# An AdaLN block with sorted experts: grouping of the last batches, v projection layout, transfers per step, and order of the maximum's scores

## The chip, the cores and the metric

The kernel runs on one core of a Trainium2 chip. The metric is the device time of one execution in microseconds (us). The kernel before has a median of 872.28 us over 9 runs (868.27 to 878.45).

## The reference

For 16 batches of 512 tokens with 128 features, in float32, the block computes an adaptive layer norm, windowed attention, a second adaptive layer norm and a mixture of experts:

```python
h = layernorm(x) * (1 + ca) + sa            # ca, sa, ga, cb, sb, gb: per batch, from silu(c) @ wmod
x = x + ga * attention(h)                   # 16 heads of 8, keys within +-32 of the query, softmax
h = layernorm(x) * (1 + cb) + sb
scores = softmax(h @ gate_w.T)              # 8 experts, the best 2 of each token
routed = sum over the 2 of w2[e]( silu((s*h) @ w1[e]) * ((s*h) @ w3[e]) )
shared = ( silu(h @ w1s) * (h @ w3s) ) @ w2s
x = x + gb * (shared + routed)
```

## The kernel before

One instruction stream per engine is written out by hand, in the order in which the Python code emits it (a manual schedule). The main loop has 64 steps, four per batch; step (b, u) handles 128 queries.

**A step** does this. `weights` makes the transposed scores t (key by query) of this step in two PSUM tiles, and ScalarE (ACT) takes their exponential. `average` multiplies the weights of the step before with the values (`v_own`) into the unused columns of a score tile. `transposed(n + 1)` turns the next step's shifts (`neg`). `look_ahead(n + 3)` calls `row_max`: it computes the query-by-key scores s for the step three ahead, VectorE (DVE) takes their maximum (L402), and GpSimd (POOL) cuts it into three bf16 pieces (L410, L412). `divided` turns the average (`raw`, L471) and divides it. Between these calls, `between(b, u, 0..3)` puts in everything else by a table `places`: the projections of batch b+2 (`project`), the values of batch b+1 (`project_v`), the output projection, second norm, logits and shared expert of the batches before (`finish`, seven stages), and the three beats of the expert stream.

**PSUM.** t, s and the experts' `uv` tiles rotate through one pool of three tiles (`ps_s`); a new tile takes the one that came free first.

**Sorted experts.** The batches of a group (`GROUPS`, three at a time) are routed together (`route`): each token's two choices get positions in a table in HBM that is sorted by expert, in tiles of 128 rows. `scatter` writes the scaled rows there with indirect transfers issued by POOL, 8 per batch. The table is then worked off in quads of four tiles (`quads_of`: 8 quads for three batches, 6 for two, 4 for one). A quad has five parts: SyncE (SP) fetches its rows (`xg`, 256 KB) and four times one expert's matrices (`wg`, 4 x 192 KB); `beat_a` turns the rows (xT); `beat_b` multiplies them with w1 and w3 (`uv`) and gates; `beat_c` multiplies with w2 (`ye`) and stores the result from ACT's queue. Two quads are fetched ahead; `wg` and `xg` have three buffers each, so that a fetch waits for the `ye` or the xT of the quad three before. When a group's last quad is done, `combine` gathers the results, 8 indirect transfers per batch (`yg`, four buffers), adds them to what `finish` has stored, and stores the sum (L824).

**Budget of indirect transfers.** `window` lets POOL issue two pairs of transfers per step, scatters first. The first transfer of a window waits until ACT has copied `raw` of this step, so that the transfers of a step follow each other in one run.

**Unsorted batches.** Batches 14 and 15 are in no group: `scores_of` spreads their scores, and each of their units is one expert over all 512 tokens (`scaled`, `gated`, `added`): 9 units per batch, the shared expert among them.

**The tail.** After the last step a loop works in rounds: one quad and one unit per round, two calls of `tick` (finishing, routing, four indirect transfers, one call of `combining`). A round's order on TensorE (PE) is xT of the next quad, the unit's broadcast of scores (b), uv of this quad, uv of the unit (`uv_all`), ye of the quad before, `sums` of the unit before.

**Values.** `project_v` makes, for each of eight blocks of 64 queries, the values of 128 keys that begin 64 after each other: eight matmuls of 128 rows per batch, each row of keys computed twice. Two ACT copies per batch (L369) spread them into `v_own`.

Of the kernel before, what the change touches and what calls it, by code (L numbers as in the profile page):

```python
# [10 lines left out]
F32 = mybir.dt.float32  # L11
# [21 lines left out]
EPS = 1e-5  # L33
SCALE = DH ** -0.5
NEG = -1e30
GROUPS = (3, 3, 3, 3, 2)
SORTED = sum(GROUPS)
MAX_T = 4 * max(GROUPS)
QUAD = 4
# [11 lines left out]
def adaln_block(ctx: ExitStack, tc: tile.TileContext, x, wq, bq, wk, bk, wv, bv, wo, bo,  # L51
# [92 lines left out]
    pieces_of = [const.tile([P, 4, G, 32], BF16, name=f"pieces{n}") for n in range(NPC)]  # L144


    NVO = 3
    v_own_of = [const.tile([P, 2, 4 * 8 * 32 + 16], F32, name=f"v_own{n}") for n in range(NVO)]
    smallT = const.tile([P, 27], F32, name="smallT")
    modT = const.tile([P, 6, B], F32, name="modT")  # L150
    wT = [const.tile([P, D], F32, name=f"wT{n}") for n in range(4)]
# [23 lines left out]
    with ExitStack() as c1:  # L175
# [5 lines left out]
        def misc(name):  # L181
            return ps_m.tile([P, 512], F32, tag="m", name=name)
# [65 lines left out]
        def zero_but_ones(t):  # L248
            nc.gpsimd.memset(t, 0.0)
            nc.gpsimd.memset(  # L250
                t[:, :, 0 : 4 * 8 * 32].rearrange("p s (m c) -> p s m c", c=32)[:, :, :, DH : DH + 1], 1.0
            )

        def operands():
# [5 lines left out]
        def more_operands():  # L260
            for t in pieces_of[2:]:
                nc.gpsimd.tensor_copy(t.rearrange("p i g r -> p (i g r)"), pieces_0)
            zero_but_ones(v_own_of[2])
            nc.gpsimd.memset(zero, 0.0)

        def gate(t, shape, name):
# [90 lines left out]

        def project_v(b):

            m = made[b]  # L360
            hT = m.hT
            m.v_own = []
            for half in range(2):
                ps = misc(f"v_{b}_{half}")
                for n in range(4):
                    i = half * 4 + n
                    mm(ps[:, n * D : (n + 1) * D], hT[:, i * QB : i * QB + P], wvT)
                t = v_own_of[(2 * b + half) % NVO]
                nc.scalar.copy(  # L369
                    t[:, :, 0 : 4 * 8 * 32].rearrange("p s (m c) -> p m s c", c=32)[:, :, :, 0:DH],  # L370
                    ps.rearrange("p (m s c) -> p m s c", s=2, c=DH),
                )
                m.v_own += [(t.rearrange("p s c -> p (s c)"), 8 * n) for n in range(4)]
                yield

        def edge(u):
# [72 lines left out]
        def average(b, u, w, v_own):  # L449

            t = spare.pop() if spare else ps_s.tile([P, 2, 512], F32, tag="s", name=f"o_{b}_{u}")
            spare.clear()
            w = w.rearrange("p g (a h j q) -> p g a h j q", a=2, h=2, j=J)
            for a in range(2):
                c = slice(4 * KM + a * QB, 4 * KM + (a + 1) * QB)
                v, m0 = v_own[2 * u + a]
                for s in range(2):
                    for n in range(2):
                        for g in range(G):
                            k0 = s * 4 * 8 * 32 + (m0 + 2 * g + n) * 32  # L460
                            mm(t[32 * g : 32 * g + 32, n, c], v[:, k0 : k0 + 32], w[:, g, a, :, 2 * n + s, :],
                               start=s == 0, stop=s == 1)
            raw = wk_p.tile([P, 2, U], F32, tag="raw", name=f"raw_{b}_{u}", bufs=2)
            nc.scalar.copy(raw, t[:, :, 4 * KM : 4 * KM + U])
            return raw
# [233 lines left out]
        def scatter(g):  # L699


            r = sorts[g]
            r.stored = []

            def scaled_rows(b, k):

                rows = wk_p.tile([P, NT, D], F32, tag="rows", name=f"rows_{b}_{k}", bufs=2)
                n0 = (b - first_of[g]) * NT
                nc.vector.tensor_tensor(
                    rows, h2_of[b], r.top[:, k, n0 : n0 + NT].unsqueeze(2).to_broadcast([P, NT, D]), ALU.mult  # L710
                )
                return rows

            todo = [(b, k) for b in range(first_of[g], first_of[g] + GROUPS[g]) for k in range(2)]
            ahead = scaled_rows(*todo[0])
            yield
            for i, (b, k) in enumerate(todo):
                rows, n0 = ahead, (b - first_of[g]) * NT
                for t in range(NT):
                    while t % 2 == 0 and not two_free():  # L720
                        yield

                    nc.gpsimd.memset(apart, 0.0)
                    stored = nc.gpsimd.indirect_dma_start(  # L724
                        out=table[g % 2][:, :],
                        out_offset=bass.IndirectOffsetOnAxis(ap=r.pos[:, k, n0 + t : n0 + t + 1], axis=0),
                        in_=rows[:, t, :], in_offset=None,
                    ).ins
# [7 lines left out]
        sorts, scatters = {}, []  # L736
        n_places, window = [0], []

        def two_free():

            if not window:
                return False
            raw = window.pop()
            if raw is not None:
                nc.gpsimd.tensor_copy(apart, raw[0:1, 0, 0:1])
            return True
# [47 lines left out]
        def combined(g, b):  # L794

            r = sorts[g]
            ys = []
            for k in range(2):
                y = None
                for t in range(NT):  # L800
                    while t % 2 == 0 and not two_free():
                        yield
                    if y is None:
                        y = wk_p.tile([P, NT, D], F32, tag="yg", name=f"yg_{b}_{k}", bufs=4)
                    s = (b - first_of[g]) * NT + t
                    nc.gpsimd.indirect_dma_start(  # L806
                        out=y[:, t, :], out_offset=None, in_=result[g][:, :],
                        in_offset=bass.IndirectOffsetOnAxis(ap=r.pos[:, k, s : s + 1], axis=0),
                    )
# [12 lines left out]
            yield  # L822
            yield
            nc.sync.dma_start(out=x_dram, in_=xb)  # L824

        def combine(g):

            active, todo, n = [], list(range(first_of[g], first_of[g] + GROUPS[g])), 0
            while active or todo:
                if todo and n % 4 == 0:  # L830
                    active.append(combined(g, todo.pop(0)))
                n += 1
                active = [a for a in active if next(a, 0) is None]
                yield
# [34 lines left out]
            nc.vector.tensor_tensor(flat, ps, flat, ALU.add)  # L869
            nc.sync.dma_start(out=out[b].rearrange("(t p) d -> p t d", p=P), in_=xs[b])  # L870

        every, sums = [], []

        FETCH = 2
        stream = [(g, q) for g, nb in enumerate(GROUPS) for q in range(quads_of(nb))]
# [100 lines left out]
        def between(b, u, n):  # L976
            for f in places.get((u, n), []):
                f(b)
            if n < 3 or b == B - 1:
                routing()  # L980
            if n == 0 and raw_of:
                window[:] = [None, raw_of[-1]]
                scattering()
                combining()
                window.clear()
            n_places[0] += 1
            fetch_some()
# [16 lines left out]
        with tc.manual_schedule():  # L1004
# [21 lines left out]
            for n, (b, u) in enumerate(steps):  # L1026
# [7 lines left out]
                transposed(n + 1)  # L1034
                other_half()
                between(b, u, 0)
                if pending is not None:
                    divided(pending, raw)
                if n == 0:
                    projecting(1)  # L1040
                between(b, u, 1)
                if n == 0:
                    projecting(1)
                look_ahead(n + AHEAD)
                between(b, u, 2)
                if n < 3:
                    next(once, None)
# [11 lines left out]
            sums += [t[:, n, :] for n in range(2)]  # L1059
            x_next = h_last = None  # L1060
            stores = []

            def tick():
                for b in range(B - 3, B):
                    finishing(b)
                routing()
                window[:] = [None, None]
                scattering()
                combining()
                window.clear()  # L1070
                n_places[0] += 2
                fetch_some()
# [102 lines left out]
```

## Time and profile before

| | |
|---|---|
| median of 9 runs | 872.28 us |
| the profiled execution: its own time, its span | 875.78 us, 873.7 us |
| PE, DVE, ACT, POOL busy | 699.8, 442.7, 423.3, 426.1 us |
| mean granted TensorE clock | 0.909 |
| last step's t scores on PE | from 689.9 us |
| matmuls of the last quad's `ye` | at 832.3 us |
| last indirect transfer, last store | at 865.5 us, 870.3 us |

Times in the views are microseconds from the start of the span; a line like L402 is a line of the kernel's file. L62 is the helper through which all matmuls go, so its groups are told apart by their tiles. An arrow `a <- b` in a tile name reads "a is written from b"; `[3.6 <-X]` behind an instruction is the idle time of its engine before it and what ended it. "Another core or an unknown queue" and "remote" stand where the profile sees no releaser.

### The profile page before, as it was taken

The numbers are of one execution on the slowest core, as the hardware profiler recorded it, in microseconds if no ns is written. First come the engines' busy times: TensorE is split into PE (matmuls) and PEld (weight loads), VectorE is DVE, ScalarE is ACT, GpSimd is POOL, SyncE is SP. The second block draws the span as 40 slices with busy tenths as digits, with TensorE's granted clock in tenths as the row PEclk, the third lists the DMA queues.
The fourth block names the chain that finished last, engine by engine and source line by source line (L and its number), as shares of the span: only waits on it lengthen the run. The fifth ranks groups of instructions, "written<-read, shape, count | busy, mean of one in ns | idle before, by whom it ended". The sixth has DMA issues, their size and how long they took to land.

```text
span 873.7 us, 26167 instructions
## 1 busy us (share of the span) xinstructions
PE 699.8 (80%) x10792; PEld 524.2 (60%) x10792; DVE 442.7 (51%) x1058; ACT 423.3 (48%) x733; POOL 426.1 (49%) x934
## 2 busy tenths in 40 slices
PE   5889999877898888988988897788977655786980
PEld 3567676655676666766766776576765543554630
DVE  3444656744558253447635254653536452754482
ACT  3667777554675454745554555444542412332310
POOL 3533334486533555446556564454464647333355
PEclk9899999999999898998899899887997778898896
DMA  5080310112423524360553345345414344666634
GB/s 166 2 228 26 89 31 14 47 32 66 127 73 87 145 82 133 89 174 25 148 151 107 109 126 149 95 109 149 119 54 133 111 154 123 183 198 192 199 108 110
DMA packets 119509, 97.49 MB, mean 112 GB/s; under 512 B 9124, under 2 KB 113486, under 8 KB 119390
## 3 DMA queue, kind: packets, MB, share of 16 engines
q1 hardware_dynamic: 91834, 70.70, 29.1%
q0 software_dynamic: 7168, 14.69, 5.8%
q10 hardware_dynamic: 20388, 10.43, 4.1%
q8 instruction: 84, 1.38, 0.6%
q14 instruction: 35, 0.29, 0.1%
HBM read 66.39 MB, written 30.97 MB: 111 GB/s over the span
## 4 chain that ended last, share of the span: by engine, by line
PE 47%; DVE 14%; issue 14%; ACT 10%; another core or an unknown queue 6%; POOL 4%; DMA 2%; SPq 1%; DVEq 0%; ACTq 0%; POOLq 0%
PE s L62 12%; PE t L62 10%; PE uv L62 5%; DVE neg L402 3%; ACT w L444 2%; PE q L62 2%; POOL yg L806 2%; PE uv_sh L62 2%; PE ye L62 2%; PE lg L62 2%; PE v L62 2%; PE raw L471 2%; PE ys L62 2%; PE xT L211 2%
## 5 line engine op out<-in xcount | busy, mean ns | idle before, releaser
L444 ACT ACTIVATE w<-t 128x1024 f32<-128x1024 f32 x128 | 131.6, 1028 | 77.0 <-PE t L62 74.4
L806 POOL DMA_INDIRECT yg<-result,r_posi x112 | 110.6, 987 | 92.1 <-DVE yg L819 45.5
L402 DVE TENSOR_REDUCE neg<-s 128x8 f32<-128x768 f32 x128 | 116.7, 952 | 56.5 <-remote 22.0
L410 POOL CAST pieces<-neg 128x16 bf16<-128x16 f32 x192 | 56.1, 292 | 161.8 <-DVE neg L402 151.6
L724 POOL DMA_INDIRECT table<-rows,r_posi x112 | 112.3, 1002 | 26.3 <-issue 25.5
L62 PEld LDWEIGHTS s<-w,v_own 128*32 128x32 f32 x3904 | 67.2, 119 | 44.4 <-issue 31.3
L62 PE MATMUL s<-w,v_own 128*32 128x64 f32 x3904 | 81.1, 234 | 9.9 <-issue 9.6
L62 PE MATMUL t<-q_own,kT 32*128 32x256 f32 x1024 | 84.0, 437 | 0.0
L62 PEld LDWEIGHTS <-packed 32*128 32x128 bf16 (+2 forms) x1101 | 33.0, 97 | 82.8 <-issue 67.0
L62 PE MATMUL uv<-xT,wg 128*128 128x128 f32 x608 | 81.8, 292 | 0.0
L62 PEld LDWEIGHTS uv<-xT,wg 128*128 128x128 f32 x608 | 77.6, 207 | 5.7 <-issue 4.4
L474 DVE RECIPROCAL rec<-raw 128x16 f32<-128x16 f32 x64 | 16.2, 253 | 121.3 <-PE raw L471 121.3
L62 PE MATMUL s<-kT,q_own 32*128 32x96 f32 x2048 | 70.3, 271 | 3.4 <-issue 2.2
L62 PEld LDWEIGHTS s<-kT,q_own 32*128 32x128 f32 x2048 | 69.2, 191 | 4.2 <-issue 4.2
L555 DVE SCALAR_TENSOR_TENSOR g<-g,uv 128x512 f32<-128x512 f32 x38 | 26.1, 686 | 77.4 <-ACT g L554 37.2
L62 PEld LDWEIGHTS t<-q_own,kT 32*128 32x128 f32 x1024 | 58.5, 219 | 3.9 <-issue 0.4
L62 PE MATMUL t<-packed 32*128 32x256 bf16 x512 | 36.4, 299 | 26.7 <-DVE neg L402 18.9
L554 ACT ACTIVATE g<-uv 128x512 f32<-128x512 f32 x38 | 22.7, 598 | 67.7 <-PE uv L62 28.2
L774 ACT COPY xT<-xT 128x512 f32<-128x512 f32 x38 | 22.2, 585 | 62.4 <-PE xT L211 37.4
L211 PE MATMUL xT<-wide,xg 128*128 128x128 f32 x152 | 27.4, 301 | 25.0 <-DMA xg<-table 14.1
L195 POOL TENSOR_SCALAR veps_f<-mv_f 128x4 f32<-128x4 f32 x16 | 5.7, 356 | 82.5 <-DVE mv_f L191 82.5
L62 PE MATMUL ye<-wg,h 128*128 128x128 f32 x304 | 43.0, 286 | 0.2 <-DVE xe L843 0.2
(188 smaller groups left out, 1351.2 us busy)
## 6 DMA issues: line engine op xcount, KB each, us to landing
wg<-experts SPq DMA_DIRECT2D x152, 192.0 KB
xg<-table SPq DMA_DIRECT2D x38, 256.0 KB
result<-ye ACTq DMA_DIRECT2D x38, 256.0 KB
mb<-mod_rows SPq DMA_DIRECT2D x16, 320.0 KB
x<-in_L_attn_x_dram SPq DMA_DIRECT2D x16, 256.0 KB
table<-zero SPq DMA_DIRECT2D x8, 512.0 KB
out_dram<-x SPq DMA_DIRECT2D x16, 256.0 KB
xb<-out_dram SPq DMA_DIRECT2D x14, 256.0 KB
```

Of the source, the lines that this page charges most:

```text
L62: nc.tensor.matmul(o, lhsT, rhs, start=start, stop=stop)
L211: nc.tensor.transpose(ps[:, t * P : (t + 1) * P], src[:, t, :], ident)
L402: nc.vector.tensor_reduce(neg[:, :, 2 * n : 2 * n + 2].rearrange("p i g -> p g i"), tiles[n][:, :, 0 : 4 * KM].rearrange("p g (i k) -> p g ...
L410: nc.gpsimd.tensor_copy(pieces[:, :, :, n], neg)
L444: nc.scalar.activation(w[:, 2 * n : 2 * n + 2, :], tiles[n], AF.Exp, scale=SCALE)
L471: nc.tensor.transpose(ps[:, n * P : (n + 1) * P], raw[:, n, :], ident)
L474: nc.vector.reciprocal(rec, both[:, :, DH])
L554: nc.scalar.activation(a, t[:, 0, :], AF.Tanh, scale=0.5)
L555: nc.vector.scalar_tensor_tensor(a, a, 1.0, t[:, 0, :], ALU.add, ALU.mult)
L724: stored = nc.gpsimd.indirect_dma_start(out=table[g % 2][:, :], out_offset=bass.IndirectOffsetOnAxis(ap=r.pos[:, k, n0 + t : n0 + t + 1], ...
L774: nc.scalar.copy(xT, ps)
L806: nc.gpsimd.indirect_dma_start(out=y[:, t, :], out_offset=None, in_=result[g][:, :], in_offset=bass.IndirectOffsetOnAxis(ap=r.pos[:, k, s ...
```

## The change

Six edits come together.

1. `GROUPS` gets a sixth group of one batch. Batch 14 is routed, scattered, worked off in four quads, and combined; only batch 15 goes through all experts. The tail has 9 units in place of 18 and four quads more, and batch 14's shared expert is done by `finish`.
2. The values are computed without the overlap: five matmuls per batch (four of 128 rows and one of 64) in place of eight. Three copies per part (six per batch) lay them out in two tiles, one for even and one for odd blocks; the tiles are smaller and there are four.
3. The combined results are stored from ACT's queue, one call of `combining` later.
4. A step's window allows five indirect transfers in place of two pairs; a tick of the tail allows eight in place of four.
5. In the tail a new batch is combined at every second call of `combining` in place of every fourth.
6. `look_ahead` moves from behind `between(b, u, 1)` to a place right behind `between(b, u, 0)`, ahead of `divided`.

```diff
-GROUPS = (3, 3, 3, 3, 2)
+GROUPS = (3, 3, 3, 3, 2, 1)
...
-    NVO = 3
-    v_own_of = [const.tile([P, 2, 4 * 8 * 32 + 16], F32, name=f"v_own{n}") for n in range(NVO)]
+    PAIR = 48
+    v_own_of = [const.tile([P, 4 * 8 * PAIR], F32, name=f"v_own{n}") for n in range(4)]
...
-            m.v_own = []
-            for half in range(2):
-                ps = misc(f"v_{b}_{half}")
-                for n in range(4):
-                    i = half * 4 + n
-                    mm(ps[:, n * D : (n + 1) * D], hT[:, i * QB : i * QB + P], wvT)
-                t = v_own_of[(2 * b + half) % NVO]
+            even, odd = (v_own_of[(2 * b + n) % 4] for n in range(2))
+            m.v_own = [((even, odd)[i % 2], 8 * (i // 2)) for i in range(2 * NU)]
+
+            def put(t, p0, k, ps, p1, n, rows):
+
+                m0, m1 = 8 * k, 8 * (k + n.stop - n.start)
                 nc.scalar.copy(
-                    t[:, :, 0 : 4 * 8 * 32].rearrange("p s (m c) -> p m s c", c=32)[:, :, :, 0:DH],
-                    ps.rearrange("p (m s c) -> p m s c", s=2, c=DH),
+                    t[p0 : p0 + rows].rearrange("p (m k c) -> p m k c", k=3, c=16)[:, m0:m1, 0:3:2, 0:DH],
+                    ps[p1 : p1 + rows, n.start * D : n.stop * D].rearrange("p (m s c) -> p m s c", s=2, c=DH),
                 )
-                m.v_own += [(t.rearrange("p s c -> p (s c)"), 8 * n) for n in range(4)]
+
+            for k0, k1 in ((0, 3), (3, 5)):
+                ps = misc(f"v_{b}_{k0}")
+                for k in range(k0, k1):
+                    r = min(P, SP - k * P)
+                    mm(ps[0:r, (k - k0) * D : (k - k0 + 1) * D], hT[:, k * P : k * P + r], wvT)
+                last = min(k1, NT)
+                put(even, 0, k0, ps, 0, slice(0, last - k0), P)
+                put(odd, 0, k0, ps, QB, slice(0, last - k0), QB)
+                first = max(k0, 1)
+                put(odd, QB, first - 1, ps, 0, slice(first - k0, k1 - k0), QB)
                 yield
...
-                    while t % 2 == 0 and not two_free():
+                    while not one_free():
                         yield
...
             yield
             yield
-            nc.sync.dma_start(out=x_dram, in_=xb)
+            yield
+
+            nc.scalar.dma_start(out=x_dram, in_=xb)
...
-                if todo and n % 4 == 0:
+                if todo and n % apart_by[0] == 0:
...
-                window[:] = [None, raw_of[-1]]
+                window[:] = [None] * 4 + [raw_of[-1]]
...
                 between(b, u, 0)
+                if n == 0:
+                    projecting(1)
+                    projecting(1)
+                look_ahead(n + AHEAD)
                 if pending is not None:
                     divided(pending, raw)
-                if n == 0:
-                    projecting(1)
                 between(b, u, 1)
-                if n == 0:
-                    projecting(1)
-                look_ahead(n + AHEAD)
                 between(b, u, 2)
...
+            apart_by[0] = 2
...
-                window[:] = [None, None]
+                window[:] = [None] * 8
```

`two_free` is renamed `one_free`; `average` and the zeroing of `v_own` follow the new layout.

More of the change, by code (lines that the diff above doesn't have):

```diff
@@ L250, in zero_but_ones @@
             nc.gpsimd.memset(
-                t[:, :, 0 : 4 * 8 * 32].rearrange("p s (m c) -> p s m c", c=32)[:, :, :, DH : DH + 1], 1.0
+                t.rearrange("p (m k c) -> p m k c", k=3, c=16)[:, :, 0:3:2, DH : DH + 1], 1.0
             )
@@ L262, in more_operands @@
                 nc.gpsimd.tensor_copy(t.rearrange("p i g r -> p (i g r)"), pieces_0)
-            zero_but_ones(v_own_of[2])
+            for t in v_own_of[2:]:
+                zero_but_ones(t)
             nc.gpsimd.memset(zero, 0.0)
@@ L459, in average @@
                         for g in range(G):
[L460 removed]
+                            k0 = (m0 + 2 * g + n) * PAIR + s * 16
                             mm(t[32 * g : 32 * g + 32, n, c], v[:, k0 : k0 + 32], w[:, g, a, :, 2 * n + s, :],
@@ L737, in adaln_block, with one_free @@
         n_places, window = [0], []
-        def two_free():
+        def one_free():
             if not window:
@@ L800, in combined @@
                 for t in range(NT):
-                    while t % 2 == 0 and not two_free():
+                    while not one_free():
                         yield
@@ L870, in stored @@
             nc.sync.dma_start(out=out[b].rearrange("(t p) d -> p t d", p=P), in_=xs[b])
-        every, sums = [], []
+        every, sums, apart_by = [], [], [4]
         FETCH = 2
```

## The prediction

> **What bounds the kernel now.** I read the page first: TensorE (PE) is busy in eight or nine tenths of a slice while the 64 steps run, and less from slice 32 on.
>
> ```profile
> PE 699.8 (80%) x10792; PEld 524.2 (60%) x10792; DVE 442.7 (51%) x1058; ACT 423.3 (48%) x733; POOL 426.1 (49%) x934
> PE   5889999877898888988988897788977655786980
> DMA  5080310112423524360553345345414344666634
> ```
>
> Then the same by stretches, which separates two regimes. In the last full 97 us of the loop PE is the bound with few gaps. In the tail it is busy for 32.5 of 48 us, and the DMA share is higher (fields: length, then PE, weight loads, DVE, ACT, POOL busy, clock, DMA share, GB/s).
>
> ```profile
> 600.00:697.00 97.00, 77.76 (x1288) 61.86 (x1279) 46.16 (x112) 43.29 (x74) 52.42 (x111) 0.86 0.38 110
> 712.00:760.00 48.00, 32.52 (x178) 24.19 (x178) 22.33 (x59) 12.07 (x25) 25.31 (x32) 0.86 0.55 162
> 760.00:800.00 40.00, 32.26 (x170) 22.57 (x170) 19.65 (x30) 11.11 (x20) 14.51 (x15) 0.91 0.73 211
> ```
>
> The waits of PE from 100 to 690 us say what a moved score can remove.
>
> ```profile
> PE t L62 <- DVE neg L402: 18.3, 18, 3.8
> PE raw L471 <- ACT raw L464: 8.2, 15, 2.5
> PE raw L471 <- ACT w L444: 4.9, 1, 4.9
> PE t L62 <- DVE h L557: 2.3, 5, 0.6
> ```
>
> The chain of waits has pieces without a releaser, nine of 3.2 to 4.7 us in the loop (34.7 us together). Beside POOL's timeline each ends about 0.8 us behind a run of indirect transfers; here is one, from the chain and then the timeline.
>
> ```profile
> 436.15 3.60 another core or an unknown queue
> ```
> ```profile
> 437.94 0.96 POOL L724 DMA_INDIRECT table<-rows,r_posi  x1 [0.21 <-issue]
> 439.77 0.59 ACT L774 COPY xT<-xT 128x512 f32<-128x512 f32 x1 [3.63 <-remote]
> ```
>
> The tail's timeline gives its rounds. The uv of quads 3_0 to 3_4 (group, quad) begin at 695.8, 713.1, 718.0, 730.3 and 746.1 us, those of the next nine up to 824.7, 8.73 us apart.
>
> ```profile
> 706.09 0.60 PE L62 MATMUL scT<-packed,r_pieces 128*24 128x128 bf16 x4 [7.92 <-DVE r_pieces L622]
> 746.06 3.52 PE L62 MATMUL uv<-xT,wg 128*128 128x128 f32 x16
> 776.77 6.96 SPq L767 DMA_DIRECT2D wg<-experts  x4
> 784.20 0.51 SPq L752 DMA_DIRECT2D xg<-table  x1
> 788.25 1.08 PE L211 MATMUL xT<-wide,xg 128*128 128x128 f32 x4 [4.44 <-DMA xg<-table]
> 824.67 2.05 PE L62 MATMUL uv<-xT,wg 128*128 128x128 f32 x16
> 865.46 0.95 POOL L806 DMA_INDIRECT yg<-result,r_posi  x1 [0.30 <-issue]
> ```
>
> A round without a wait takes 6.2 us (uv at 772.1 and 778.3). The others wait for rows that SP issues only behind the four weight loads, which wait for `ye` three quads back. After the last quad's store (834.0) 40 us are left to the end: 24 gathers of three batches, 1.25 us apart.
>
> **The loop, part by part.** Values: the matmuls and the copy have these rows.
>
> ```profile
> L62 PE MATMUL v<-wT,hT x256: 275/275/527, 18.3 to 652.5; 128*128 128x128 f32 x128
> L369 ACT COPY v_own<-v x32: 586/586/617, 19.5 to 653.4; 128x512 f32<-128x512 f32 x32
> ```
>
> Four matmuls take 1.12 us in the chain's pieces (1.08 to 1.16), 0.28 each. Three fewer in 16 batches are 13.4 us of PE. The chain holds 2% of the span (17.5 us) of their 35.8 us, half; so I take half, **-6.6** (0 to -13.4). Copies: raw's 256 columns take 0.37 us, 512 take 0.586, so about 0.15 + 0.00085 per column; 24 partitions take 0.57 for 512 (scT), so half the partitions save nothing. Widths 384, 384, 256 and 128, 128, 256 make 2.2 us per batch against 1.17: 16.5 us more on ACT, which is half idle. Behind them wait the gate and the exponentials; the chain has 10% of ACT, so **+2** (0 to +5).
>
> Moved scores: the maximum is ready earlier, and raw's transposes no longer stand at the head while ACT copies. That can remove 18.3 + 8.2 + 4.9 = 31.4 us. But uv now comes last before the next t, which takes over its PSUM tile in the built order of allocations. t then waits for tanh 0.6 and two DVE operations of 0.69, about 2.2 us with hand-overs; 0.55 of xT always lies between, with u = 0 and 2 more. With an exposed wait of 0.7 us on some 40 gated tiles of the loop it gives back 28 us. Net **-4** (-31 to +45, the latter 40 x 1.65 less the 20.6 of the first and last row).
>
> Five transfers: runs grow from 4 x 1.27 to 6.35 us, and from about 37 to 30 in number. If 9 of 37 still stall the chain, now 1.27 us longer, that is 30 x 0.243 x (3.85 + 1.27) = 37.4 against 34.7, with short new ones **+4** (-35 if the pieces have another cause that goes, +38 if all 30 pay). POOL's pieces, queued behind a run, are due two steps later, so they stay hidden; with that cover gone they would cost 1.4 us a step. One consequence: scattering ends one step earlier, and one quad more is done within the loop: uv 1.8, ye 0.9, xT 0.5, **+3.2** (0 to 3.2).
>
> The runs rest on a row, where the Trainium skill (DMA: Bandwidth & Descriptors, Issuing engines are not separate DMA queues) says that transfers of all issuers interleave on the same 16 engines. By that alone a longer run would hold nobody up, the +4 would be 0, and the forecast 858.5.
>
> Stores on ACT: 14 issues of 0.39 us leave SP; ACT gets 15 and can wait for the DVE add, with exponentials behind it. One call of distance covers that; taken as nothing (0 to +6). Zeroing: 1.83 us for 2080 columns becomes about 1.35 for 1536, beside 5.8 us in which POOL idles; nothing. Loop: -6.6 + 2 - 4 + 4 + 3.2 = **-1.4**.
>
> **The tail.** Where uv of 3_0 stood (695.8), 3_1 now stands; sixteen quads follow in place of thirteen. In the built order the transposed scores scT of batch 14 are gone from PE's queue, with the 7.92 us before them; part comes back, since batch 14's routing on DVE now stands ahead of batch 15's last division. The first four rounds: 50.3 - 7.9 = 42.4. Then eight rounds with a unit at 8.73 = 69.8, and four without, 8.73 less uv_all's 1.75, 7.0 each: 28. Queue of SP: batch 8's old sum is loaded (L815) into the buffer of batch 6, whose store ACT now issues a round later; the next rows stand behind it, +3 (0 to 5). After the last uv: 6.5 to the store's issue (9.3 before, with a unit between), 2.5 to land (bounds 1.7, a gather's, and 5.2, the slowest xg), eight gathers 10.0, landing 1.7, three DVE operations 2.2, store and end 3.4: 26.3. End: 695.8 + 42.4 + 69.8 + 28 + 3 + 26.3 = 865.3 against 873.7, **-8.4**. The eight scatters and the 20 small DVE operations of batch 14's routing lie beside these rounds.
>
> The loads' rows are 3.7 and 3.9 us from issue to landing in the chain (xg, 256 KB), up to 5.2. The Trainium skill (DMA: Bandwidth & Descriptors, Anatomy of one DMA) fits 2.0 us plus bytes over 436 GB/s, an estimate of 2.6; by it each of six pairs of rounds would be 1.2 us shorter and the forecast 855.3.
>
> **Sum.** -1.4 - 8.4 = -9.8 on the profiled execution's 875.78 gives 866.0. That execution lies 3.5 us above the median; on 872.28 the forecast is **862.5**. What a measurement can tell from no change is 0.5%, 4.4 us.
>
> **Rivals.** *Rounds at PE's own pace.* With nine units gone and the stores off SP's queue, the twelve later rounds take 6.2 and 4.5 us: 67.6 in place of 97.8, 30 us less, 832. For it: two such rounds exist. Against it: nothing in the fetch's chain gets shorter. *One wait for another.* If t waits 0.7 us on the 40 tiles and raw's two waits only move elsewhere, the moved scores cost 28 - 20.6 = 7.4 in place of -4: 874, no change. For it: ACT and DVE come between uv and t in either order. Against it: DVE has less queued ahead of the gate's two operations than ahead of the maximum. *Runs of five hold the engines up.* One mechanism, in the loop: every step's run of transfers blocks whoever needs the unknown queue until it ends. At 0.75 us more for each of 30 runs it costs 22.5 in place of 4: 881, slower. It decides from 0.6 us per run on (9.8 + 4.4 + 4, over 30). For it: nine pieces that end with runs, and in the tail ACT, DVE and SP standing still until 742 behind a run that ends at 741. Against it: three of four runs cost nothing now.
>
> **How the numbers follow.** Forecast 0.48, own range 850 to 873; PE's pace 0.14; one wait for another 0.20; runs of five 0.18. Faster: most of the forecast's 0.48, 0.14 and a little of the third: 0.62. Same: 0.20. Slower: 0.18. The range, 842 to 882, goes beyond the forecast's own toward both outer rivals; it leaves out most of PE's pace below (0.1) and about half of the runs of five above (0.09).
>
> **What would show it.** Right: 160 v matmul records in place of 256; t's wait for the maximum gone, a wait for h of 0.5 to 0.8 us in its place; 3_1's uv in the last step; dense rounds near 8.7; eight gathers and 26 us behind the last uv. Wrong: pieces without a releaser that sum to over 50 us in the loop; t waiting for h over 30 us; a last uv before 820 or after 845.

## The result, and the profile after

The changed kernel takes 995.28 us (median of 20 runs, 984.51 to 998.93) against 871.5 us of the kernel before (62 runs): ratio 1.1446, 95% interval 1.1422 to 1.147, so 14.5% slower where 1% faster was forecast. Its profiled execution has a span of 993.3 us against 873.7; that of the kernel before lies 0.5% over its median, so differences of a few us between the two profiles say nothing.

Where the loss lies follows from the first exponential of each batch (`w<-t`). From batch 0 to batch 4, with no transfer of rows yet, 126.4 us against 114.9; from batch 4 to batch 15, 587.2 against 513.4; from there to the end 246.9 against 212.7. That is +11.5, +73.8 and +34.2 us.

The page after, first engines and PE's slices: PE does 13 us more in 120 us more.

```profile
PE 712.6 (72%) x10755; PEld 537.7 (54%) x10755; DVE 437.1 (44%) x1058; ACT 443.7 (45%) x799; POOL 432.4 (44%) x956
PE   5889888767888767878576877868667750674841
```

The same by stretches (length, PE, weight loads, DVE, ACT, POOL, clock, DMA share, GB/s): a stretch of the loop, and one of the tail with PE busy for a third of it.

```profile
600.00:697.00 97.00, 75.45 (x1094) 58.02 (x1091) 43.19 (x102) 45.06 (x81) 46.56 (x96) 0.83 0.35 100
800.00:848.00 48.00, 16.20 (x91) 14.91 (x92) 14.29 (x41) 7.03 (x15) 31.25 (x42) 0.64 0.43 125
```

PE's waits from 100 to 780 us (what for, us in total, times, longest). The wait of t for the maximum, which the moved scores were to remove, grew from 18.3 to 31.5, and waits for the division (`o`) and the gate (`h`) came to it.

```profile
PE t L62 <- DVE neg L414: 31.5, 8, 5.9
PE h2T L212 <- DVE o L487: 16.1, 5, 4.9
PE t L62 <- DVE h L569: 14.3, 9, 2.4
```

The chain (start, length, what): pieces without a releaser sum to 65.5 us before 735 us (34.7 in the loop before), and the tail has one piece of 29 us.

```profile
670.89 14.73 another core or an unknown queue
809.94 29.25 issue
```

The step just ahead of the first of these two pieces shows in the timeline what such a piece is: the scores are through at 661.3, the last transfer of POOL's run ends at 665.7, and only then DVE begins the maximum and ACT the gate's tanh.

```profile
660.24 1.03 PE L62 MATMUL s<-kT,q_own 32*128 32x96 f32 x32
664.72 0.96 POOL L736 DMA_INDIRECT table<-rows,r_posi  x1 [0.23 <-issue]
666.66 1.82 DVE L414 TENSOR_REDUCE neg<-s 128x8 f32<-128x768 f32 x2 [11.33 <-PE xT L212]
666.93 0.60 ACT L566 ACTIVATE g<-uv 128x512 f32<-128x512 f32 x1 [6.17 <-PE xT L212]
```

I call such a wait *held*: an ACT or DVE instruction that starts over 1 us after everything has ended that it waits for (the built program names the semaphores, the trace the times; waits that include a transfer are left out). By this count the kernel before has 44 of them (102 us), the changed one 49 (168 us); all but one fall into a run of indirect transfers or the 2.5 us behind it, and most end 0.7 to 1.4 us behind the run.

### The profile page after: what moved, and what is told of

The parts are those of the page before. It is cut to its first block, busy times and chain, and to the rows that moved or that the text cites. A ratio compares the mean times of both kernels' runs of the same rounds, so it can differ in the third digit from the quotient of the medians.

```text
span 993.3 us, 26361 instructions
## 1 busy us (share of the span) xinstructions
PE 712.6 (72%) x10755; PEld 537.7 (54%) x10755; DVE 437.1 (44%) x1058; ACT 443.7 (45%) x799; POOL 432.4 (44%) x956
## 3 DMA queue, kind: packets, MB, share of 16 engines
q8 instruction: 84, 1.38, 0.6%
## 4 chain that ended last, share of the span: by engine, by line
PE 45%; DVE 16%; issue 12%; another core or an unknown queue 8%; ACT 7%; DMA 5%; SPq 3%; POOL 2%; DVEq 0%; POOLq 0%; ACTq 0%
PE s L62 11%; PE t L62 9%; DVE neg L414 5%; PE uv L62 5%; PE ye L62 2%; DMA xg<-table 2%; PE q L62 2%; PE uv_sh L62 2%; PE ys L62 2%; PE raw L483 1%; ACT w L456 1%; PE neg L62 1%; SPq L778 1%; DMA table<-rows,r_posi 1%
## 5 line engine op out<-in xcount | busy, mean ns | idle before, releaser
L818 POOL DMA_INDIRECT yg<-result,r_posi x120 | 117.9, 982 | 122.7 <-DMA wg<-experts 70.9
L736 POOL DMA_INDIRECT table<-rows,r_posi x120 | 119.8, 999 | 30.6 <-issue 26.7
L422 POOL CAST pieces<-neg 128x16 bf16<-128x16 f32 x192 | 50.6, 264 | 181.3 <-DVE neg L414 170.5
L62 PEld LDWEIGHTS uv<-xT,wg 128*128 128x128 f32 x672 | 91.6, 217 | 23.3 <-issue 15.8
L62 PE MATMUL uv<-xT,wg 128*128 128x128 f32 x672 | 97.9, 303 | 8.1 <-issue 5.0
L62 PE MATMUL t<-q_own,kT 32*128 32x256 f32 x1024 | 88.5, 463 | 0.0
L62 PEld LDWEIGHTS <-packed 32*128 32x128 bf16 (+1 forms) x1098 | 32.9, 98 | 96.6 <-issue 80.2
L62 PE MATMUL t<-packed 32*128 32x256 bf16 x512 | 36.0, 320 | 47.2 <-DVE neg L414 31.5
L62 PE MATMUL ye<-wg,h 128*128 128x128 f32 x336 | 49.0, 292 | 13.1 <-DVE h L569 11.3
L62 PEld LDWEIGHTS ye<-wg,h 128*128 128x128 f32 x336 | 44.2, 202 | 18.8 <-DVE h L569 11.0
L212 PEld LDWEIGHTS xT<-wide,xg 128*128 128x128 f32 x168 | 20.1, 147 | 59.3 <-issue 51.7
```

The costliest lines, as they stand in the source:

```text
L62: nc.tensor.matmul(o, lhsT, rhs, start=start, stop=stop)
L212: nc.tensor.transpose(ps[:, t * P : (t + 1) * P], src[:, t, :], ident)
L422: nc.gpsimd.tensor_copy(pieces[:, :, :, n], neg)
L736: stored = nc.gpsimd.indirect_dma_start(out=table[g % 2][:, :], out_offset=bass.IndirectOffsetOnAxis(ap=r.pos[:, k, n0 + t : n0 + t + 1], ...
L818: nc.gpsimd.indirect_dma_start(out=y[:, t, :], out_offset=None, in_=result[g][:, :], in_offset=bass.IndirectOffsetOnAxis(ap=r.pos[:, k, s ...
```

## The experiments

The sets of runs went to different chips. The first set (e1 to e4) shows held waits like the two traces above, and in all the later runs not one is left; this is what *with holds* and *without holds* mean below. It is not the only difference: the kernel before takes 880.06 us in the first set, with a granted TensorE clock of 0.902 to 0.917, and 788 to 791 us in the others, at 0.926 to 0.942. Ratios are always against the kernel before in the same set, on the same chip. The cuts of code are shortened: a `...` stands for lines left out.

**One edit at a time, on a chip with holds.** Theory A says that the scores' new place puts the maximum's wait into the run; B that the new order costs in every batch; D that runs of five cost by themselves; C and E follow the prediction and the copies. The first cut leaves out two calls of `projecting` that move along in the very first step of the 64.

```diff
                 between(b, u, 0)
+                look_ahead(n + AHEAD)          # e1; taken back in e4
                 if pending is not None:
                     divided(pending, raw)
                 between(b, u, 1)
-                look_ahead(n + AHEAD)
```

> The kernel before with the moved scores alone (look_ahead between the calls for place 0 and the division). Theory A (held waits): in the changed kernel the maximum's wait for its scores begins while a run of indirect transfers is under way and ends only about 1 us behind the run, and everything queued behind it on DVE comes late with it; then this edit alone loses 40 to 80 us (910 to 950), nearly all of it in batches 4 to 15, in which there are transfers. Theory B (order alone): the new order costs about 2.8 us in every batch, transfers or not, as batches 0 to 3 of the changed kernel show; then this edit loses 30 to 45 us spread evenly over 16 batches (902 to 917). Theory C (the moved scores are innocent, as the prediction had it): 863 to 876.

Measured: 942.04, ratio 1.0717 (1.0642 to 1.0791). Of the stretches, batches 0 to 4 take 5.5 us more than before, 4 to 15 54 us, the tail 5. That is inside A's range, but B's cost is there too.

```diff
-                window[:] = [None, raw_of[-1]]          # two grants of two
+                window[:] = [None] * 4 + [raw_of[-1]]   # five grants of one
```

> The kernel before with five transfers a step in the loop in place of four, the tail still with four a call. Theory D (the runs of five by themselves, the rival of the prediction): most of the loop's loss of some 100 us is here, 930 to 970. Theory A (held waits, of which the moved scores put the most important one into the run): with the scores in their old place the runs are longer but fewer, so 872 to 885.

Measured: 922.83, ratio 1.0486 (1.0411 to 1.0561): above A's range and under D's. Batches 4 to 15 take 565.1 us, 51.7 more than before.

```diff
-    v_own_of = [const.tile([P, 2, 4 * 8 * 32 + 16], F32, name=f"v_own{n}") for n in range(NVO)]
+    v_own_of = [const.tile([P, 4 * 8 * PAIR], F32, name=f"v_own{n}") for n in range(4)]
...
-                            k0 = s * 4 * 8 * 32 + (m0 + 2 * g + n) * 32
+                            k0 = (m0 + 2 * g + n) * PAIR + s * 16
```

That is e3, with the new `project_v` and zeroing and nothing else of the change.

> The kernel before with the new layout of the values alone: 160 matmuls in place of 256, six copies a batch in place of two. The prediction's terms: 6.6 us less of PE, 2 more by ACT: 868. Theory E (the copies are what makes batches 0 to 3 slower by 2.8 us each): 44 us more, 916.

Measured: 877.19, ratio 0.998 (0.9942 to 1.0019). The copies are no cause (E falls); a gain of 0.2% can't be told from none.

e4 is the changed kernel with the first diff taken back.

> The changed kernel with the scores in their old place, all else as changed. Theory A: 40 to 90 us of the 123 come back, 905 to 955. Theory C or D: at most 5 come back, 990 to 1000. If the moved scores and the runs of five act together, this gains more than the moved scores lose in the kernel before.

Measured: 959.34, ratio 1.0905 (1.0834 to 1.0976). Against the changed kernel's 1.1446, which is from another set, the moved scores cost 5.4% there and 7.2% alone, so with holds they and the runs do not strengthen each other; 79 us remain without them.

**What of it goes without holds.** The next set landed on a chip without holds. e5 is e2 with a third buffer, which the units' `xe` get too, since they share the tag:

```diff
-                rows = wk_p.tile([P, NT, D], F32, tag="rows", name=f"rows_{b}_{k}", bufs=2)
+                rows = wk_p.tile([P, NT, D], F32, tag="rows", name=f"rows_{b}_{k}", bufs=3)
```

> Runs of five alone again (923 with two buffers of scaled rows), now with a third buffer for the scaled rows. With five a run crosses from one batch's rows to the next, so DVE's product for the rows after that can wait for transfers of the run that is going. Theory F (DVE stands at that product behind the run): most of the 43 us come back, 875 to 890. Theory A/D (waits of all engines that begin in a run end with it, and five transfers last 1.25 us longer than four): at most 10 come back, 912 to 925.

Measured: 780.27 against 791.48, ratio 0.9865 (0.9807 to 0.9922); the set's absolute expectations are void, since its chip is another. e11 and e14 below settle it.

```diff
-            if n == 0 and raw_of:
-                window[:] = [None, raw_of[-1]]          # two grants of two
+            if n in (0, 2) and raw_of:                  # two grants of one, twice
+                window[:] = [None, raw_of[-1] if n == 0 else None]
```

> The kernel before with the four transfers of a step split into two and two, at place 0 (behind raw, as now) and at place 2. If a wait that begins in a run is held until about 1 us behind its end, short runs hold less: two of 2.5 us hold at most 2 x (2.5 + 1), but what they hold is seldom as much as one of 5 us; 850 to 870. If it is the number of transfers that costs, or the place at the step's end is worse: 872 to 900.

Measured: 775.38, ratio 0.9788 (0.9743 to 0.9833). It is faster, but with no holds there, not for the reason given; what makes it faster was not taken apart.

```diff
-                    stored = nc.gpsimd.indirect_dma_start(
-                        out=table[g % 2][:, :],
-                        out_offset=bass.IndirectOffsetOnAxis(ap=r.pos[:, k, n0 + t : n0 + t + 1], axis=0),
-                        in_=rows[:, t, :], in_offset=None,
-                    ).ins
+                    place = (2 * n0 + NT * k + t) * P
+                    stored = nc.gpsimd.dma_start(out=table[g % 2][place : place + P, :], in_=rows[:, t, :]).ins
```

The gathers of `combined` are changed in the same way.

> The changed kernel, with every indirect transfer (rows into the table, rows out of the result) replaced by a direct one of the same 64 KB from the same queue of POOL to fixed places: the sorting of the rows is left out, the traffic stays. If the holds come from POOL's work on indirect transfers, they go, and with them most of the loop's loss in batches 4 to 15: 880 to 920. If they come from the traffic or from the order of the scores alone: 975 to 1000.

Measured: 813.76, ratio 1.0282 (1.0222 to 1.0343). Without holds on that chip it can't tell what makes them. It serves further on, for the tail.

e8 also leaves the loop's run at four transfers, as four grants of one:

```diff
-GROUPS = (3, 3, 3, 3, 2)
+GROUPS = (3, 3, 3, 3, 2, 1)
...
-            nc.sync.dma_start(out=x_dram, in_=xb)
+            yield
+            nc.scalar.dma_start(out=x_dram, in_=xb)
...
+            apart_by[0] = 2
...
-                window[:] = [None, None]
+                window[:] = [None] * 8
```

> The kernel before with batch 14 as a group of its own and the edits of the tail (eight transfers a call, batches two rounds apart, stores by ACT); the loop's runs stay four, values and scores stay as before. By the four traces the stretch from batch 15's first step to the end is 212.7 us before, 208 to 218 with one edit of the loop, and 246 to 248 wherever batch 14 is a group: 30 to 36 us of loss here, 903 to 910. If that stretch is only long because the loop's end is disturbed by runs of five: 872 to 885. The prediction's own term is a gain of 8.4: 864.

Measured: 816.23, ratio 1.0306 (1.0262 to 1.0351): 24.8 us, a loss as expected, if under the 30 to 36 us, from the tail's edits alone.

> The changed kernel once more, unedited. In the four runs before this one no wait of ACT or DVE for another engine was held longer than 1 us in a run of indirect transfers, and the kernel before took 791 us there, where it took 880 in the four runs ahead of those with many such holds: the two sets ran on different chips. So whether a chip holds waits is read from each run's own trace. Theory A (the holds are what the moved scores and the runs of five cost): with holds in the trace the ratio is 1.13 to 1.16 again, without them 1.02 to 1.05, which is the tail's part (25 us of 791 in the kernel with the tail's edits alone) and what batches 0 to 3 lose. Theory B/D (order and length of runs cost by themselves): 1.10 or more on either chip.

Measured: 870.06 against 788.75, ratio 1.1035 (1.0976 to 1.1094). No wait is held, and still 81 us are lost: A's 1.02 to 1.05 was wrong, and holds are not the main part of the 124. The same step as above, in this run's timeline, shows the maximum beginning with the scores' end, in the middle of POOL's run:

```profile
588.97 1.03 PE L62 MATMUL s<-kT,q_own 32*128 32x96 f32 x32
590.05 1.82 DVE L414 TENSOR_REDUCE neg<-s 128x8 f32<-128x768 f32 x2 [5.77 <-PE s L62]
592.20 0.60 ACT L566 ACTIVATE g<-uv 128x512 f32<-128x512 f32 x1 [2.62 <-PE uv L62]
593.64 0.96 POOL L736 DMA_INDIRECT table<-rows,r_posi  x1 [0.22 <-DVE g L567]
```

e10, e11 and e12 repeat e1, e5 and e6 beside it.

> The kernel before with the moved scores alone, once more. With holds in the trace: 1.07 as measured. Without: theory A 1.005 to 1.015 (what batches 0 to 3 lose, 1.4 us a batch, is there in every batch), theory B 1.05 or more.

Measured: 819.68, ratio 1.04 (1.0325 to 1.0474): 31 us without one hold, so A's 1.015 is too low and B's 1.05 too high. PE's waits from 60 to 600 us say where: first the run of e8, whose loop has the old order, then e10.

```profile
PE t L62 <- DVE neg L402: 14.7, 24, 2.8
PE ys L62 <- DVE h_sh L557: 6.1, 11, 0.7
PE oT L211 <- DVE o L475: 4.7, 3, 4.1
PE t L62 <- DVE h L557: 3.0, 6, 0.6
```
```profile
PE ys L62 <- DVE h_sh L557: 13.0, 10, 1.7
PE t L62 <- DVE h L557: 11.8, 15, 2.4
PE oT L211 <- DVE o L475: 11.0, 4, 4.5
PE t L62 <- DVE neg L402: 6.0, 3, 2.5
```

t's wait for the maximum does fall by 8.7 us. But ys and t wait 15.7 more for the gate: ys because it multiplies the gate's result, t because it takes over the PSUM tile of uv, which the gate reads. oT waits 6.3 more for the division; over all who wait for it, it is 20.8 us in e10 against 5.3 in e8 and 10.9 in e17 (below), whose loop has the same order as e8's. In the whole loop (batches 0 to 15) e10 takes 29 us more than e8: PE idles for 76 us against 52 and is busy for 5 more. Two reasons are possible for the new waits: the maximum's 1.9 us on DVE ahead of gate and division, or PE's order, in which the 1.2 us of scores no longer stand between a gate's matmuls and the ys or t that wait for it.

> Five transfers a step with a third buffer for the scaled rows, 0.9865 on the chip without holds. On the same chip again: 0.98 to 0.99. On a chip with holds: theory A/D 1.035 to 1.05, as with two buffers (1.0486); theory F (DVE standing at the scaled rows was the loss) 0.98 to 1.01.

Measured: 781.42, ratio 0.992 (0.9889 to 0.9951), a little over the range.

> Two and two transfers a step, 0.979 on the chip without holds. On the same chip again: 0.975 to 0.985. On a chip with holds: if a wait is held only to the end of its run, short runs hold less, 0.95 to 0.98; if the holds go with the number of runs, 1.0 to 1.03.

Measured: 777.32, ratio 0.9859 (0.9785 to 0.9932), again without holds.

**The moved scores and the runs, taken apart.**

```diff
                 between(b, u, 0)
+                scores_ahead(n + AHEAD)        # the matmuls
                 if pending is not None:
                     divided(pending, raw)
                 between(b, u, 1)
-                look_ahead(n + AHEAD)
+                maximum_ahead()                # DVE's two reductions, POOL's pieces
```

> The kernel before with the scores moved up on PE alone: their matmuls stand between the calls for place 0 and the division, the maximum over them (two reductions of 0.95 us on DVE, POOL's pieces) stays where it was. Theory G (the moved scores cost because the maximum's 1.9 us stand on DVE ahead of the division and of the gate's two products, for whose results PE waits): the loss goes, 0.99 to 1.01 in place of 1.04 (1.07 with holds). Theory H (PE's order: raw's transposes and what comes after stand behind 1.1 us of scores): 1.03 to 1.04 remain.

Measured: 825.01 against 789.96, ratio 1.0449 (1.0407 to 1.049). In time G falls and H stands: with the maximum back in its place nothing is regained. PE's waits say why (60 to 600 us):

```profile
PE t L62 <- DVE neg L403: 20.8, 28, 3.0
PE ys L62 <- DVE h_sh L558: 15.0, 10, 1.8
PE t L62 <- DVE h L558: 15.0, 15, 1.7
PE oT L211 <- DVE o L476: 5.1, 4, 4.2
```

PE waits for the gate at least as long as in e10, though the maximum no longer stands ahead of it on DVE. For this part the scores' place on PE is the cause; the likely reading is that they were the work that covered tanh and two products behind a gate's matmuls. For the division G is right in part: over all who wait for it, 12.2 us are left of 20.8. But t's wait for the maximum, which is late again, rises from 6.0 to 20.8 and takes that back. That the scores hold two of the pool's three PSUM tiles longer in e13 may cost too; it was not told apart.

e14 repeats e2.

> Runs of five with two buffers of scaled rows, 1.0486 on the chip with holds. On a chip without holds: theory F (DVE stands at the scaled rows, whose buffer is read by transfers of the same run; DVE's waits of 4 to 8 us there were seen in both kernels with five) 1.01 to 1.04 against 0.9865 and 0.992 with three buffers; theory A alone (only the holds cost) 0.985 to 0.995. With holds: 1.04 to 1.055 again.

Measured: 804.28, ratio 1.0191 (1.0141 to 1.0241), against 0.9865 and 0.992 with the third buffer, as F expects. DVE's waits from 100 to 640 us for the buffer of scaled rows, with four transfers a step (e8), with five (e14), and with five and a third buffer (e5):

```profile
DVE rows L709 <- DMA table<-rows,r_posi: 35.2, 13, 4.5
```
```profile
DVE rows L709 <- DMA table<-rows,r_posi: 47.2, 11, 8.0
```
```profile
DVE rows L709 <- DMA table<-rows,r_posi: 0.2, 1, 0.2
```

Four transfers are exactly one tile of scaled rows. With five a run reaches into the next tile, and DVE's product for the tile after that waits for transfers that POOL issues in the same run; what stands behind it on DVE waits along. The wait itself is there with four as well. With five single waits are longer, and the long ones reach PE, as here in e14:

```profile
202.52 0.69 DVE L709 TENSOR_TENSOR rows<-h,r_top 128x512 f32<-128x512 f32 x1 [7.72 <-DMA table<-rows,r_posi]
204.62 0.61 PE L62 MATMUL t<-packed 32*128 32x256 bf16 x6 [8.52 <-DVE neg L402]
```

Between 60 and 640 us PE has five waits over 5 us in e14, and four of them (8.5, 5.1, 6.9 and 5.4 us) end 1.3 to 2.6 us behind the start of such a product; e5 has two waits as long, and none behind one.

By stages the loop loses more than the total says. Batches 0 to 15 take 587.0 us in e14 and 565.3 in e5, against 558.6 in e17, whose loop is the old one (all on chips without holds). The stretch behind them takes 184.4 and 181.1 against 199.9 in e10, whose tail is the old one: with five, 48 gathers are issued before batch 15 begins, with four 36. So five transfers cost the loop 28 us with two buffers and 7 with three, and win some 15 to 19 in the tail. Four transfers with a third buffer were not run, so how much of e5's gain is the buffer's own stays open.

**The tail.** e15 is e8 with this in `tick`:

```diff
                 scattering()
-                combining()
+                if n_sorted[0] == len(GROUPS):
+                    combining()
```

> The kernel with the tail's edits alone (1.0306 without holds), with no gather put into POOL's queue in the tail until batch 14's eight transfers into the table stand there. In the run of the tail's edits, eight gathers (10.4 us) stood right ahead of batch 14's rows, and PE then waited 12.2 us for them to come back from the table. Theory T1 (the gathers ahead are the loss): 1.00 to 1.015. Theory T2 (the chain of batch 14 itself, its routing on DVE, 10 us of transfers and the load, is the loss, and the gathers only stand beside it): 1.02 to 1.035; the gathers that come later can also lengthen the end.

Measured: 814.54, ratio 1.0323 (1.0285 to 1.036): T1 falls, the gathers ahead are not the loss. PE's longest wait for the table's rows does shrink from 12.2 to 7.3 us, but the sum of these waits doesn't (30.8 in e8, 32.2 here).

e17 is the kernel before with the first line of e8's diff and nothing else:

```diff
-GROUPS = (3, 3, 3, 3, 2)
+GROUPS = (3, 3, 3, 3, 2, 1)
```

> The kernel before with batch 14 as a group of its own and nothing else: four transfers a call in the tail, batches four calls apart, stores by SP. Theory T2 (the chain of batch 14's routing, transfers and load is the loss, since 9 units less of TensorE work stand beside it): 1.025 to 1.045, as with all of the tail's edits (1.0306) or a little more. Theory T3 (the other edits of the tail lose, the group gains as predicted): 0.985 to 1.01.

Measured: 801.2 against 788.57, ratio 1.0159 (1.0113 to 1.0204): the group alone loses 12.6 us, between T2 and T3. The tail's other edits thus lose about as much again, 1.5% across two chips; they were not taken apart.

How a group loses is in PE's waits from 600 us on, first the changed kernel, then e17, then e10, whose groups and tail are those of the kernel before:

```profile
PE xT L212 <- DMA xg<-table: 38.3, 6, 23.0
```
```profile
PE xT L211 <- DMA xg<-table: 28.9, 8, 10.2
```
```profile
PE xT L211 <- DMA xg<-table: 6.4, 2, 3.2
```

In e8 it is 30.8 us, hardly more than in e17, so what the other edits lose stands elsewhere. The wait of 23.0 us lies on the 29 us piece of the chain, which ends at 839.19 with the load that PE waits for. That load is issued behind batch 14's last transfer into the table, in the timeline of the changed kernel:

```profile
836.92 0.97 POOL L736 DMA_INDIRECT table<-rows,r_posi  x1 [0.23 <-issue]
839.19 0.38 SPq L764 DMA_DIRECT2D xg<-table  x1
842.09 1.09 PE L212 MATMUL xT<-wide,xg 128*128 128x128 f32 x4 [23.00 <-DMA xg<-table]
```

That load isn't batch 14's: it is quad 3_6. There are two tables, `table[g % 2]`, so group 5 writes into the one that group 3's last quads are still read from. In the built program the load of 3_6 (of 3_5 in e8 and e15) waits for the last of the eight, as each of the eight is written as a transfer to the whole of it (`out=table[g % 2][:, :]`). All quads behind it in the stream wait too. Without holds the traces name this wait; in e17 it is SP's at this load (655 to 670 us), and PE's for its rows:

```profile
SPq L752 <- DMA table<-rows,r_posi: 9.2, 1, 9.2
```
```profile
668.46 1.09 PE L211 MATMUL xT<-wide,xg 128*128 128x128 f32 x4 [10.17 <-DMA xg<-table]
```

PE's 10.2 us at this one load are of the size of e17's whole loss. In e7, whose direct transfers name their rows, the load of 3_6 is issued at 693.2 us, ahead of the eight (698.5 on), and PE's waits for `xg` from 600 us on were 17.3 us with a longest of 9.6, against 43.0 and 23.6 in e9. Its transfers are also shorter to issue (0.54 us for 0.96), so that the shared table is the reason is supported, not proven; a third table wasn't tried.

**What a faster version takes.**

e16 joins the diffs of e3 and e6 and the third buffer of e5; e18 is e6 once more.

> What the runs so far point to: the kernel before with the new layout of the values (0.998, its loop 7 us shorter), the transfers of a step as two and two (0.979 and 0.986 without holds) and a third buffer for the scaled rows. If the three add up: 0.965 to 0.98 without holds. With holds nothing of the split is known: 0.95 to 1.02.

Measured: 780.84, ratio 0.988 (0.9838 to 0.9922): faster than both kernels, but the three do not add up: it is no faster than two and two transfers alone.

> Two and two transfers a step, 0.979 and 0.986 on two chips without holds. Without holds again 0.975 to 0.99. With holds: 0.95 to 0.98 if a wait is held only to the end of its run, 1.0 to 1.03 if the holds go with the number of runs.

Measured: 776.28 against 788.57, ratio 0.9849 (0.9806 to 0.9892). Two and two transfers a step is the best version found, 1.4 to 2.1% faster than the kernel before on three chips without holds. On a chip with holds neither it nor the third buffer was measured.

## Why the prediction was wrong, point by point

- **Values, -6.6 and +2.** The trace after has the 160 records foretold, and e3's 0.998 is compatible with the -4.6 as with nothing. Not a cause of the loss.
- **Moved scores, -4 (-31 to +45): the step that failed first.** It cost 31 us without holds and 62 with them, the latter over its own upper end. (Its two terms, 28 and 31.4, give -3.4.) The removal was real in part: t's wait for the maximum fell by 8.7 us in e10, and raw's wait for its copy, 5.4 us in e8, went. The step priced one new wait, t for h, at 0.7 us on 40 tiles, 28 us. That wait took 11.8 us in e10, so it was priced too high; what it left out was ys, which needs the shared gate (13.0 for 6.1), and the division (20.8 for 5.3). That the scores were cover behind every gate's matmuls was not seen. The rival *One wait for another* named the right kind of loss and put 7.4 on it.
- **Runs of five, +4 (-35 to +38).** The second step that failed. Without holds 14 us, and a gain of 6 to 11 with a third buffer. What it had wrong is the wait of DVE for the scaled rows' buffer, in no term and no bound by name: with four transfers single waits stay under 4.6 us, with five they go up to 8.0 and reach PE. In the loop alone five cost 28 us; with three buffers 7, near the 7.2 of +4 and +3.2, though not shown to be for their reasons. With holds 43 us, over the upper end. The rival *Runs of five hold the engines up* had the sign and the place, and 22.5 us; the prediction set three runs in four that cost nothing against its strongest evidence, the nine pieces that end with runs. Without holds the loss has another cause than the one this rival names.
- **Stores on ACT, 0.** Part of the tail's other edits, which lose some 12 us together; not told apart.
- **Tail, -8.4: the third step that failed.** It lost 24.8 us (e8), 34.2 in the profile after. That 3_1's uv stands where 3_0's stood was right (782.9, just behind the last step's start), and rounds of 7.0 to 8.0 us came from 3_7 to 4_2 (863.8 to 885.9). What failed is the sum of rounds with no gap between them: the first four rounds, 42.4 in the sum, took 60.1 us (58.1 in e9). In them 3_5's uv follows 3_4's by 28.9 us, because it stands on PE behind the xT of 3_6, whose fetch waits for batch 14's transfers. After 4_2 two more gaps follow, 17.9 and 13.1 us, which e9 does not have. And behind the last uv 43.0 us are left (33.1 in e9) where 26.3 were added; that part was not taken apart.
- **The signs.** Pieces without a releaser 65.5 us (over 50) and the last uv at 950.3 (after 845) were named as signs of being wrong; t waiting 14.3 us for h, under the 30 named, was not. The sign of being right named for this wait, t's wait for the maximum gone, failed too: 31.5 us.

Of the 123.8 us, 81 are there without holds: moved scores 31, tail 25, runs of five 14, measured one by one on different chips; the remaining 11 were not taken apart. About 42 more come only with holds. There the held waits grow from 102 to 168 us, the maximum's from some 1.9 us on average to 3.4; that the holds make all of the 42 is not shown, since these chips differ in the clock as well.

The prediction weighed the Trainium skill's rule (DMA: Bandwidth & Descriptors, Issuing engines are not separate DMA queues) that transfers of all issuers interleave on the same 16 engines, from which it took that a longer run holds nobody up. On four chips the traces do not contradict that: no held wait, and 0.9865 with five and a third buffer. With holds it fails: a wait can last to the end of a run. The 2.6 us that the prediction worked out from that page for a load of xg rests on a fit for transfers that POOL issues; these loads are SP's, and the 3.7 and 3.9 us of the trace decide. The Trainium skill (Perfetto Trace Analysis, DMA Instruction — SWDGE (GPSIMD)) also says that the slice of such a transfer ends when its descriptors are written, not when its data is there. The traces agree: in e10 six of DVE's fourteen waits for the buffer of scaled rows ended 1.38 to 1.40 us behind the last slice before them, and none sooner (the others 1.9 to 5.2).

## What to carry to other kernels

Before a piece of PE's work is moved up because one consumer waits for it, list what it covers where it stands: the chain of ACT and DVE behind the matmuls just ahead of it becomes a wait of the next one that needs its result or its PSUM tile. Before a batch of transfers is made larger, count it in tiles of its source: here runs of five over tiles of four lost 14 us in all with two buffers and nothing with three. And before a new group shares a table with an old one, look which loads the program orders behind its transfers: here one load of the old group waited for all eight of the new.

## What the runs showed of the hardware

The same kernel takes 871.5 and 880 us where waits are held and 788 to 791 us where none is, with a granted clock of 0.902 to 0.917 in the set at 880 and 0.926 to 0.942 in the others. POOL's indirect transfers follow each other at about 1.26 us in both. With holds, waits of ACT and DVE for PE that begin in a run of POOL's indirect transfers end mostly 0.7 to 1.4 us behind it, even when the run lasts 20 us; on four others, 13 runs with such transfers show none over 1 us. What else differs between the chips, and by which path the waits are held, stays open: the run with direct transfers, meant to tell, met a chip without holds.
